# The second product of an attention kernel: seven float32 products of a 2x2 scheme, or three float32r products of 12-bit halves

## The chip, the cores and the metric

The kernel runs on one core of one Trainium2 chip. The metric is the device time of one execution in microseconds; lower is better. Input and output lie in device memory as the reference has them.

## The reference, cut to what matters

```python
x: (4, 64, 64, 256)      # B, W, H, C;  N = W*H = 4096, C2 = 128
q = einsum('bwhc,cd->bwhd', x, Wq) + bq      # C -> 128
k = einsum('bwhc,cd->bwhd', x, Wk) + bk      # C -> 128
v = einsum('bwhc,cd->bwhd', x, Wv) + bv      # C -> 256
pq, pk, pv = (t.reshape(B, -1, N) for t in (q, k, v))   # a plain reshape, no transpose
energy = einsum('bcn,bcm->bnm', pq, pk)      # 4096 x 4096 for each image, over 128
attention = softmax(energy, axis=-1)         # over m
out = einsum('bcm,bnm->bcn', pv, attention)  # 256 x 4096, over m = 4096
return gamma * out.reshape(B, W, H, C) + x   # all float32
```

For each image n are the queries, m the keys. The "first product" below is the energy, the "second product" is v times the exponentials.

## The kernel before, in words

All data is float32. A float32 matmul of the source is one call; the trace shows what it becomes.

**Projections** (class Projection, lines 99 to 166). x is loaded in 16 pieces of 128 x 2 x 256 for each image (line 78, on SyncE's queue). TensorE transposes a piece (line 122), ScalarE copies it from PSUM (line 128, tile xts), TensorE makes q and k (line 135, pieces "qk") and VectorE adds their biases (line 143) into the resident tiles pq and pk. v() (lines 150 to 166) makes a piece of v with the channels on PSUM's columns; ScalarE adds the bias (line 164).

**The order** is written out by hand (manual_schedule): each engine runs its instructions in the order of the source. Queries go in groups of 512 (NB), keys in tiles of 128; a step u is one pair of key tiles of one group, 16 steps to a group and 128 to an image. The energies (line 250: pk tile stationary, 512 queries moving) run LEAD = 18 steps ahead of the second product, so there is a buffer of 19 pairs of exponentials (ppool). ScalarE takes the exponential (line 260) without subtracting a maximum. VectorE adds the exponentials up (line 271, tile ssum); at a group's end column_sums makes the sum over the partitions by a product with ones (line 283), and reciprocals (lines 286, 300).

**The second product** (attend, line 340) uses a Strassen-like 2x2 scheme in Winograd's form: v's four blocks and the exponentials' four blocks (two key tiles, two halves of 256 queries) are combined to seven products instead of eight. left_side (lines 236 to 243, GpSimd) makes the combinations of v once for each image, right_side (lines 305 to 319, VectorE) those of the exponentials in each step. The left side is stationary (128 x 128), the right one moves (256 columns). The second half of the queries is scaled by a ratio w of the column sums before (line 312), so that the two halves can be mixed. Seven sums accumulate in four PSUM banks over the 16 steps of a group. finish (lines 351 to 380) copies them (line 354, ScalarE), combines them, scales by gamma over the column sum (line 376), adds x (line 378) and writes the result on GpSimd's queue (line 379). It is a generator whose pieces are handed out by proceed(), two in each step.

The image after is projected (project_qk) in the last 18 steps of an image, in which no energies are left to make; v follows in the lead-in of the next one, between its energies. At the end, four VectorE operations (lines 409 to 412) test the column sums against bounds (Z_LOW, Z_HIGH, line 62), and a general branch (from line 416, with the maximum subtracted) would compute everything again where they don't hold.

Of the kernel before, what the change touches and what calls it, by code (L numbers as in the profile page):

```python
# [8 lines left out]
F32 = mybir.dt.float32  # L9
I32 = mybir.dt.int32  # L10
AF = mybir.ActivationFunctionType
# [6 lines left out]
def kernel(  # L18
# [43 lines left out]
    Z_LOW, Z_HIGH = 2.0**-30, 2.0**90  # L62
# [36 lines left out]
    class Projection:  # L99
# [50 lines left out]
        def v(self, i):  # L150
            pool, tag = self.psum
            vp = pool.tile([P, KC, C], F32, tag=tag, name=f"v_{self.b}_{i}")
            for eh in range(KC):
                for k in range(KC):
                    nc.tensor.matmul(  # L155
                        vp[:, eh, :],
                        wv_sb[:, k, eh * P : (eh + 1) * P],
                        self.xt[i][:, k].rearrange("p s a -> p (s a)"),
                        start=(k == 0),
                        stop=(k == KC - 1),  # L160
                    )
            to = self.v_out(i)
            for eh in range(KC):
                nc.scalar.activation(  # L164
                    to[:, eh, :], vp[:, eh, :], AF.Identity, bias=bv_sb[:, eh : eh + 1]
                )

    NB = 512
    HB = NB // 2
    NG = N // NB  # L170
    NP = NM // 2
    STEPS = NG * NP
    LEAD = NP + 2


    M2, M1, M3, M5, M6, M7, M4 = ((k // 2, k % 2) for k in range(7))
    SLOTS = [slice(0, 5, 4), slice(2, 4), slice(5, 7), slice(1, 2)]
    again = const.tile([P, 1], I32, name="again")

    zsum = const.tile([P, 2, B * NG, 2], F32, name="zsum")  # L180

    with ExitStack() as fast:
# [4 lines left out]
        xpool, qkv, apool = pool("xpool", 4), pool("qkv", 1), pool("apool", 1)  # L187

        ppool = pool("ppool", LEAD + 1)
        bpool, work, stat = pool("bpool", 2), pool("work", 1), pool("stat", 2)  # L190
        ps_s = pool("ps_s", 4, space=PSUM)
        ps_m = pool("ps_m", 1, space=PSUM)

        images, pairs, sides, left, now = [], {}, {}, {}, {}
        recip, scale = {}, {}
# [11 lines left out]
        def image(b):  # L207
            def xt_out(i):
                if i % 2 == 0:
                    now["xt"] = ppool.tile([P, 2, KC, 2, P], F32, tag="p", name=f"xts_{b}_{i}")  # L210
                return now["xt"][:, i % 2]

            def v_out(i):
                left[b, i] = apool.tile([P, 7, P], F32, tag=f"a{i}", name=f"a_{b}_{i}")
                return left[b, i][:, 0:4, :].rearrange("p (h s) c -> p h (s c)", h=2)

            pr = Projection(b, xpool, qkv, (ps_s, "s"), xt_out, v_out)
            images.append(pr)
            return pr

        def project_qk(b):
            pr = image(b)
            pr.transposed(0)
            for i in range(NI):
# [3 lines left out]
                yield  # L228

        def project_v(b):  # L230
            for i in range(NI):
                images[b].v(i)
                left_side(left[b, i])
                yield

        def left_side(a):


            tt = nc.gpsimd.tensor_tensor
            tt(a[:, 4, :], a[:, 1, :], a[:, 3, :], ALU.add)  # L240
            tt(a[:, 5, :], a[:, 4, :], a[:, 0, :], ALU.subtract)  # L241
            tt(a[:, 1, :], a[:, 0, :], a[:, 1, :], ALU.subtract)
            tt(a[:, 6, :], a[:, 2, :], a[:, 5, :], ALU.subtract)

        def energy(b, u, h):

            g, t = divmod(u, NP)
            pr = images[b]
            sp = ps_s.tile([P, NB], F32, tag="s", name=f"s_{b}_{u}_{h}")
            nc.tensor.matmul(  # L250
                sp,
                pr.pk[:, 2 * t + h, :],
                pr.pqf[:, g * NB : (g + 1) * NB],
                start=True,
                stop=True,
            )
            if h == 0:

                pairs[b, u] = ppool.tile([P, 2, 2, HB], F32, tag="p", name=f"p_{b}_{u}")
            nc.scalar.activation(  # L260
                pairs[b, u][:, h].rearrange("p f n -> p (f n)"), sp, AF.Exp
            )

        def running_sum(b, u):
            g, t = divmod(u, NP)
            flat = lambda u: pairs[b, u].rearrange("p h f n -> p h (f n)")
            if t == 0:
                now["sum"] = work.tile([P, 2, NB], F32, tag="ssum", name=f"ssum_{b}_{g}")
            else:
                q = flat(u - 1) if t == 1 else now["sum"]  # L270
                nc.vector.tensor_tensor(now["sum"], q, flat(u), ALU.add)  # L271
            if t == NP - 1:
                start(column_sums(b, g, now["sum"]))

        def column_sums(b, g, ssum):
            n = b * NG + g
            first, second = slice(0, HB), slice(HB, NB)
            z = work.tile([P, NB], F32, tag="z", name=f"z_{b}_{g}")
            nc.vector.tensor_tensor(z, ssum[:, 0, :], ssum[:, 1, :], ALU.add)
            yield  # L280
            yield
            zb = ps_s.tile([P, NB], F32, tag="s", name=f"zb_{b}_{g}")
            nc.tensor.matmul(zb, ones, z, start=True, stop=True)  # L283

            r2 = work.tile([P, HB], F32, tag="r2", name=f"r2_{b}_{g}")
            nc.vector.reciprocal(r2, zb[:, second])  # L286
            w = stat.tile([P, HB], F32, tag="w", name=f"w_{b}_{g}")
            nc.vector.tensor_tensor(w, zb[:, first], r2, ALU.mult)  # L288
            recip[b, g] = r = stat.tile([P, HB], F32, tag="r", name=f"r_{b}_{g}")
            scale[b, g] = w  # L290

            def total(j, f, t):
                nc.scalar.activation(  # L293
                    z[:, :HB], t, AF.Identity, accum_out=zsum[:, j, n, f : f + 1]
                )

            total(0, 0, zb[:, first])
            total(0, 1, zb[:, second])
            yield
            nc.vector.reciprocal(r, zb[:, first])  # L300
            total(1, 1, r2)
            yield
            total(1, 0, r)

        def right_side(b, u):

            p = pairs[b, u]
            w = scale[b, u // NP].unsqueeze(1).to_broadcast([P, 2, HB])  # L310
            tt = nc.vector.tensor_tensor
            tt(p[:, :, 1, :], p[:, :, 1, :], w, ALU.mult)  # L312
            q = bpool.tile([P, 4, HB], F32, tag="q", name=f"q_{b}_{u}")

            tt(q[:, 0:2, :], p[:, :, 1, :], p[:, 0, :, :], ALU.subtract)  # L315

            tt(q[:, 2, :], q[:, 1, :], p[:, 0, 0, :], ALU.add)  # L317
            tt(q[:, 3, :], q[:, 2, :], p[:, 1, 0, :], ALU.subtract)  # L318
            sides[b, u] = q

        def attend(b, u, part):
            g, t = divmod(u, NP)
            if t == part == 0:
                now["acc"] = [
                    ps_m.tile([P, 2, HB], F32, tag=f"m{k}", name=f"m{k}_{b}_{g}")
                    for k in range(4)
                ]
            p, q, a = pairs[b, u], sides[b, u], left[b, t]
            products = [
                (M2, 2, p[:, 1, 0, :]),  # L330
                (M1, 0, p[:, 0, 0, :]),
                (M3, 6, p[:, 1, 1, :]),
                (M5, 4, q[:, 0, :]),
                (M6, 5, q[:, 2, :]),
                (M7, 1, q[:, 1, :]),
                (M4, 3, q[:, 3, :]),
            ]
            for (bank, half), s, right in products[4 * part : 4 * part + 4]:

                nc.tensor.matmul(  # L340
                    now["acc"][bank][:, half, :],
                    a[:, s, :],
                    right,
                    start=(t == half == 0),
                    stop=(t == NP - 1),
                    skip_group_check=True,
                )
            if t == NP - 1 and part:
                start(finish(b, g, now["acc"]))

        def finish(b, g, acc):
            m = work.tile([P, 7, HB], F32, tag="m", name=f"msb_{b}_{g}")
            for bank, to in enumerate(SLOTS):
                nc.scalar.copy(m[:, to, :], acc[bank][:, : 1 if bank == 3 else 2, :])  # L354
            xr = []
            for f in range(2):
                t = xpool.tile([P, 2, XB], F32, tag="x", name=f"xr_{b}_{g}_{f}")
                nc.sync.dma_start(t, xv[b, 2 * g + f])
                xr.append(t)
            yield  # L360
            yield
# [180 lines left out]
```

## Time and profile before

| | |
|---|---|
| median of 3 runs | 2733.33 us (2733.29 to 2736.7) |
| the profiled execution's own time | 2733.03 us |
| its span in the profile | 2731.0 us, at a mean granted TensorE clock of 0.999 |
| data moved | 34.21 MB read, 16.78 MB written, 19 GB/s over the span |

The profile's engines: PE is TensorE's matmuls, PEld its weight loads, which are recorded apart, DVE is VectorE, ACT ScalarE, POOL GpSimd, SP SyncE; a name with a q behind it is the engine's queue of other instructions, and where a row names it, the issuer of a DMA. A row of a group has the line, the engine, the operation, out<-in by the program's names, the shapes (partitions x elements), how many there are, their busy time in us with the mean ns of one, then the idle time of the engine just before them and what ended most of it. A row of the timeline has the start in us, the length in us and what ran; equal instructions that follow one another are merged to one row with their count. A row of the waits has who waited for whom, us in total, times, and the longest. A row of the DMA issues ends with the KB of one and the median us from issue to landing. Matmuls are pipelined: a record lasts longer than the distance to the next one.

### The profile page before, as it was taken

What the parts mean: (1) busy time and instruction counts of PE and PEld (TensorE: products, weight loads), DVE (VectorE), ACT (ScalarE), POOL (GpSimd) and SP (SyncE); (2) the same over time, 40 slices, a digit from 0 to 9 for tenths busy, and PEclk for the clock granted to TensorE, in tenths of its full rate; (3) what the DMA queues carried; (4) which work ended last, traced back from release to release, by engine and by line L of the source; (5) the groups of instructions that cost most, each with busy time, mean ns of one, the idle gap of its engine ahead of it and who ended that gap; (6) DMA issues with size and microseconds to landing.
All of it is one profiled execution on the core that took longest, in us unless ns stands there. A gap on an engine that the chain in (4) does not pass through costs nothing.

```text
span 2731.0 us, 28069 instructions
## 1 busy us (share of the span) xinstructions
PE 2708.1 (99%) x10560; PEld 1982.2 (73%) x10560; DVE 2045.2 (75%) x3077; ACT 804.3 (29%) x1601; POOL 170.9 (6%) x326
## 2 busy tenths in 40 slices
PE   9999999999999999999999999999999999999998
PEld 6677777778767777777876777777787677777776
DVE  3687778887568777788756887778865788877787
ACT  3422322231342322232133222222213332223220
POOL 1200000000220000000022000000003100000000
PEclk9999999999999999999999999999999999999999
DMA  2000000001100000000100000000020000000000
GB/s 87 1 12 4 16 16 16 16 16 59 35 0 16 8 8 16 16 16 16 62 31 1 16 16 5 12 16 16 16 66 27 1 16 16 12 4 16 16 16 17
DMA packets 41614, 52.86 MB, mean 19 GB/s; under 512 B 3584, under 2 KB 37376, under 8 KB 41472
## 3 DMA queue, kind: packets, MB, share of 16 engines
q1 hardware_dynamic: 34816, 33.56, 4.0%
q0 software_dynamic: 5120, 16.78, 1.5%
q8 instruction: 85, 1.39, 0.2%
q10 hardware_dynamic: 1536, 0.66, 0.1%
q14 instruction: 57, 0.47, 0.1%
HBM read 34.21 MB, written 16.78 MB: 19 GB/s over the span
## 4 chain that ended last, share of the span: by engine, by line
PE 77%; issue 21%; POOL 0%; ACT 0%; DVE 0%; DMA 0%; POOLq 0%; SPq 0%; ACTq 0%
PE m L340 42%; PE s L250 25%; PE qk L135 4%; PE v L155 4%; PE xt L122 1%; PE zb L283 1%; POOL out_dram L379 0%; DVE r L286 0%; DMA x<-in_x_dram 0%; ACT a L164 0%; ACT z L293 0%; ACT xts L128 0%; DVE w L288 0%; ACT L128 0%; POOL a L241 0%
## 5 line engine op out<-in xcount | busy, mean ns | idle before, releaser
L260 ACT ACTIVATE p<-s 128x512 f32<-128x512 f32 x1024 | 606.0, 599 | 1367.8 <-PE s L250 1298.6
L340 PE MATMUL m<-q,a 128*128 128x256 f32 x4096 | 972.2, 379 | 0.0
L250 PE MATMUL s<-pq,pk 128*128 128x512 f32 x2048 | 961.0, 592 | 0.0
L340 PEld LDWEIGHTS m<-q,a 128*128 128x128 f32 x4096 | 778.2, 190 | 117.8 <-issue 13.4
L340 PEld LDWEIGHTS m<-p,a 128*128 128x128 f32 x3072 | 581.6, 190 | 272.8 <-issue 198.3
L271 DVE TENSOR_TENSOR ssum<-ssum,p 128x1024 f32<-128x1024 f32 x448 | 562.7, 1256 | 272.0 <-ACT p L260 272.0
L340 PE MATMUL m<-p,a 128*128 128x256 f32 x3072 | 746.9, 379 | 3.2 <-ACT msb L354 3.2
L250 PEld LDWEIGHTS s<-pq,pk 128*128 128x128 f32 x2048 | 389.1, 190 | 274.8 <-issue 245.9
L315 DVE TENSOR_TENSOR q<-p 128x512 f32<-128x512 f32 x512 | 355.1, 694 | 212.7 <-PE m L340 189.5
L312 DVE TENSOR_TENSOR p<-p,w 128x512 f32<-128x512 f32 x512 | 349.9, 683 | 1.1
L318 DVE TENSOR_TENSOR q<-q,p 128x256 f32<-128x256 f32 x512 | 219.2, 428 | 17.6
L317 DVE TENSOR_TENSOR q<-q,p 128x256 f32<-128x256 f32 x512 | 218.1, 426 | 17.4
L379 POOL DMA_DIRECT2D out_dram<-xr x64 | 44.2, 690 | 2404.8 <-DVE xr L378 2143.7
L155 PEld LDWEIGHTS v<-xts,wv_sb 128*128 128x128 f32 x512 | 96.9, 190 | 44.6 <-ACT a L164 18.4
L135 PE MATMUL qk<-wqk_sb,xts 128*128 128x256 f32 x512 | 122.9, 384 | 1.9 <-ACT xts L128 1.9
L155 PE MATMUL v<-xts,wv_sb 128*128 128x256 f32 x512 | 121.4, 380 | 2.7 <-ACT a L164 2.7
L286 DVE RECIPROCAL r<-zb 128x256 f32<-128x256 f32 x32 | 56.3, 1758 | 70.1 <-PE zb L283 70.1
L135 PEld LDWEIGHTS qk<-wqk_sb,xts 128*128 128x128 f32 x512 | 93.7, 192 | 13.5 <-ACT xts L128 3.0
L128 ACT COPY xts<-xt 128x512 f32<-128x512 f32 x64 | 37.3, 589 | 191.4 <-PE xt L122 191.4
L354 ACT COPY msb<-m 128x512 f32<-128x512 f32 (+1 forms) x128 | 59.0, 536 | 85.9 <-PE m L340 85.9
L164 ACT ACTIVATE a<-v,bv_sb 128x256 f32<-128x256 f32 x128 | 53.6, 470 | 65.8 <-PE v L155 65.8
L143 DVE TENSOR_TENSOR pq<-qk,bqk_sb 128x256 f32<-128x256 f32 x64 | 27.1, 424 | 55.5 <-PE qk L135 55.1
(36 smaller groups left out, 660.0 us busy)
## 6 DMA issues: line engine op xcount, KB each, us to landing
x<-in_x_dram SPq DMA_DIRECT2D x64, 256.0 KB, 2.9
xr<-in_x_dram SPq DMA_DIRECT2D x64, 256.0 KB, 2.8
out_dram<-xr POOLq DMA_DIRECT2D x64, 256.0 KB, 2.4
wv_sb<-in_L_conv_Wv_dram ACTq DMA_DIRECT2D x1, 256.0 KB, 5.2
wqk_sb<-in_L_conv_Wq_dram ACTq DMA_DIRECT2D x1, 128.0 KB, 2.1
wqk_sb<-in_L_conv_Wk_dram ACTq DMA_DIRECT2D x1, 128.0 KB, 3.2
bqk_sb<-in_L_conv_bq_dram ACTq DMA_DIRECT2D x1, 64.0 KB, 5.6
bqk_sb<-in_L_conv_bk_dram ACTq DMA_DIRECT2D x1, 64.0 KB, 6.0
```

The source lines that it names most:

```text
L135: nc.tensor.matmul(qk[:, s, :], self.xt[i][:, k, s, :], wqk_sb[:, k, :], start=(k == 0), stop=(k == KC - 1),)
L155: nc.tensor.matmul(vp[:, eh, :], wv_sb[:, k, eh * P : (eh + 1) * P], self.xt[i][:, k].rearrange("p s a -> p (s a)"), start=(k == 0), stop= ...
L250: nc.tensor.matmul(sp, pr.pk[:, 2 * t + h, :], pr.pqf[:, g * NB : (g + 1) * NB], start=True, stop=True,)
L260: nc.scalar.activation(pairs[b, u][:, h].rearrange("p f n -> p (f n)"), sp, AF.Exp)
L271: nc.vector.tensor_tensor(now["sum"], q, flat(u), ALU.add)
L286: nc.vector.reciprocal(r2, zb[:, second])
L312: tt(p[:, :, 1, :], p[:, :, 1, :], w, ALU.mult)
L315: tt(q[:, 0:2, :], p[:, :, 1, :], p[:, 0, :, :], ALU.subtract)
L317: tt(q[:, 2, :], q[:, 1, :], p[:, 0, 0, :], ALU.add)
L318: tt(q[:, 3, :], q[:, 2, :], p[:, 1, 0, :], ALU.subtract)
L340: nc.tensor.matmul(now["acc"][bank][:, half, :], a[:, s, :], right, start=(t == half == 0), stop=(t == NP - 1), skip_group_check=True,)
L354: nc.scalar.copy(m[:, to, :], acc[bank][:, : 1 if bank == 3 else 2, :])
```

## The change

The diff takes out the 2x2 scheme (left_side, right_side, running_sum, column_sums, the long lead and its buffers) and computes the second product from halves. Each number x of the exponentials is split into h, a copy scaled by just under 1 and written as float32r (a 4-byte type whose values are cut to 12 bits of mantissa when an engine writes them), and what is left of it. v is split in the same way. With E = 2^-12 the four half products are got from three sums, by Karatsuba's identity: a = sum of h*vh and of l*vl (vl is scaled by 1/E), b = sum of d*vd with d = h*E - l and vd = (v - vh)/E - vh. Then a*(1 + E) + b is the whole product.

The exponentials are now stationary (128 keys x 128 queries) and v moves (256 channels). vh and vl have two columns of ones behind the 256 channels, so that column 256 of a is the column sum. A group is 256 queries (NB = 256), a unit u four key tiles; there are 16 groups of 8 units for each image. The energies run LOOK = 2 units ahead; their matmuls stay float32 and move 256 columns. For each unit ScalarE makes two exponentials of 128 x 512 and the cut copy of 128 x 1024, VectorE two passes over 128 x 1024 (l and d). Four accumulators (a and b for each of two blocks of 128 queries) take one PSUM bank each, once. As the result now has the queries on the partitions, finish transposes it by four TensorE transposes before x is added.

Each image is projected as a whole before its energies, with v's piece three behind q and k's (LAG = 3). The bounds Z_LOW and Z_HIGH become 2^-60 and 2^80, and the test at the end adds a small product with ones over the partitions. The general branch stays as it was.

The diff, cut to its core (the lines marked + are added; what they replace is printed above):

```diff
+            v4 = now["v4"]
+            h = vh[:, m, :C]
+            nc.scalar.activation(h, v4, AF.Identity, scale=UPPER * E)
+            for t, f in ((vl, 1.0 / E), (vd, 1.0 / E + 1.0)):
+                nc.vector.scalar_tensor_tensor(
+                    t[:, m, :C], h.bitcast(F32), -f, v4, ALU.mult, ALU.add
+                )
...
+        def energy(b, u):
+            g, t = divmod(u, NU)
+            pr = images[b]
+            x = ppool.tile([P, 4, NB], F32, tag="x", name=f"x_{b}_{u}")
+            for k in range(2):
+                sp = ps_s.tile([P, 2, NB], F32, tag="s", name=f"s_{b}_{u}_{k}")
+                for i in range(2):
+                    nc.tensor.matmul(sp[:, i, :], pr.pk[:, 4 * t + 2 * k + i, :],
+                        pr.pqf[:, g * NB : (g + 1) * NB], start=True, stop=True)
+                nc.scalar.activation(x[:, 2 * k : 2 * k + 2, :], sp, AF.Exp)
+            h = ppool.tile([P, 4, NB], F32R, tag="h", name=f"h_{b}_{u}", bufs=LOOK + 1)
+            nc.scalar.activation(h, x, AF.Identity, scale=UPPER)
+        def halves(b, u):
+            x, h = units[b, u]
+            l = ppool.tile([P, 4, NB], F32R, tag="l", name=f"l_{b}_{u}")
+            nc.vector.tensor_tensor(l, x, h.bitcast(F32), ALU.subtract)
+            d = ppool.tile([P, 4, NB], F32R, tag="d", name=f"d_{b}_{u}")
+            nc.vector.scalar_tensor_tensor(
+                d, h.bitcast(F32), 1.0 + E, x, ALU.mult, ALU.subtract)
+        def attend(b, u):
...
+            for j in range(NJ):
+                a, bb = now["acc"][j]
+                for i in range(4):
+                    m = 4 * t + i
+                    n = slice(j * P, (j + 1) * P)
+                    for out_, left, right, first, last in (
+                        (a, h, vh, True, False),
+                        (a, l, vl, False, True),
+                        (bb, d, vd, True, True),
+                    ):
+                        nc.tensor.matmul(out_, left[:, i, n], right[:, m, :],
+                            start=(m == 0 and first), stop=(m == NM - 1 and last))
+        def finish(b, g, acc):
+            xr = load_x(xpool, b, g)
...
+            for j in range(NJ):
+                a, bb = acc[j]
+                nc.vector.tensor_copy(z[:, j : j + 1], a[:, C : C + 1])
+                nc.vector.reciprocal(r[:, 0, j : j + 1], z[:, j : j + 1])
+                nc.vector.tensor_tensor(r[:, 0, j : j + 1], r[:, 0, j : j + 1], gam, ALU.mult)
+                nc.vector.tensor_scalar(r[:, 1, j : j + 1], r[:, 0, j : j + 1], 1.0 + E, None, ALU.mult)
+                nc.scalar.activation(o[:, j, :], bb, AF.Identity, scale=r[:, 0, j : j + 1])
+                nc.vector.scalar_tensor_tensor(
+                    o[:, j, :], a[:, :C], r[:, 1, j : j + 1], o[:, j, :], ALU.mult, ALU.add)
+            yield
+            yield
+            tp = ps_s.tile([P, 2, NB], F32, tag="s", name=f"ot_{b}_{g}")
+            for s in range(2):
+                for j in range(NJ):
+                    nc.tensor.transpose(
+                        tp[:, s, j * P : (j + 1) * P], o[:, j, s * P : (s + 1) * P], ident)
+            nc.vector.tensor_tensor(xr, xr, tp, ALU.add)
+            nc.gpsimd.dma_start(ov[b, g], xr)
+        for b in range(B):
+            image(b)
+            pr = images[b]
             pr.transposed(0)
             for i in range(NI):
                 if i + 1 < NI:
                     pr.transposed(i + 1)
                 pr.qk(i)
+                if i >= LAG:
+                    project_v(b, i - LAG)
+                proceed()
+            energy(b, 0)
+            for i in range(NI - LAG, NI):
+                project_v(b, i)
+            for u in range(1, LOOK):
+                energy(b, u)
+            halves(b, 0)
+            for u in range(STEPS):
+                if u + LOOK < STEPS:
+                    energy(b, u + LOOK)
+                proceed()
+                if u + 1 < STEPS:
+                    halves(b, u + 1)
+                attend(b, u)
+                proceed()
```

More of the change, by code (lines that the diff above doesn't have):

```diff
@@ L9 @@
 F32 = mybir.dt.float32
+F32R = mybir.dt.float32r
 I32 = mybir.dt.int32
@@ L161, in v @@
                     )
-            to = self.v_out(i)
+            to, bias, scale = self.v_out(i)
             for eh in range(KC):
                 nc.scalar.activation(
-                    to[:, eh, :], vp[:, eh, :], AF.Identity, bias=bv_sb[:, eh : eh + 1]
-                )
-    NB = 512
-    HB = NB // 2
+                    to[:, eh, :],
+                    vp[:, eh, :],
+                    AF.Identity,
+                    bias=bias[:, eh : eh + 1],
+                    scale=scale,
+                )
+    NB = 256
+    NJ = NB // P
     NG = N // NB
[L171 to L177, printed above, removed]
+    NU = NM // 4
+    STEPS = NG * NU
+    LOOK = 2
+    LAG = 3
+    E = 2.0**-12
+    UPPER = 1.0 - 2.0**-13
     again = const.tile([P, 1], I32, name="again")
-    zsum = const.tile([P, 2, B * NG, 2], F32, name="zsum")
+    zall = const.tile([P, B * NG, NJ], F32, name="zall")
+    bv4_sb = const.tile([P, KC], F32, name="bv4_sb")
+    nc.scalar.mul(bv4_sb, bv_sb, 1.0 / E)
     with ExitStack() as fast:
@@ L218, in image, with project_v @@
[L218 to L222, printed above, removed]
+                now["v4"] = work.tile([P, KC, C], F32, tag="v4", name=f"v4_{b}_{i}")
+                return now["v4"], bv4_sb, 1.0 / E
+            images.append(Projection(b, xpool, qkv, (ps_s, "s"), xt_out, v_out))
+        def project_v(b, i):
+            images[b].v(i)
+            v4 = now["v4"]
+            m = slice(2 * i, 2 * i + 2)
+            h = vh[:, m, :C]
[4 more added lines that the diff above has]
+                )
@@ new lines, in halves @@
+        def halves(b, u):
[4 more added lines that the diff above has]
+            nc.vector.scalar_tensor_tensor(
+                d, h.bitcast(F32), 1.0 + E, x, ALU.mult, ALU.subtract
+            )
+            units[b, u] = h, l, d
+        def attend(b, u):
+            g, t = divmod(u, NU)
+            if t == 0:
+                now["acc"] = [
+                    (
+                        ps_o.tile([P, C + 2], F32, tag=f"a{j}", name=f"a{j}_{b}_{g}"),
+                        ps_o.tile([P, C], F32, tag=f"b{j}", name=f"b{j}_{b}_{g}"),
+                    )
+                    for j in range(NJ)
+                ]
+            h, l, d = units[b, u]
+            for j in range(NJ):
[8 more added lines that the diff above has]
+                    ):
+                        nc.tensor.matmul(
+                            out_,
+                            left[:, i, n],
+                            right[:, m, :],
+                            start=(m == 0 and first),
+                            stop=(m == NM - 1 and last),
+                        )
+            if t == NU - 1:
+                start(finish(b, g, now["acc"]))
@@ L227, in project_qk @@
                 pr.qk(i)
[L228 to L349, printed above, removed]
@@ L382 @@
-        for _ in project_qk(0):
-            pass
-        for b in range(B):
-            values = project_v(b)
-            for u in range(-LEAD, STEPS):
-                if u == STEPS - LEAD:
-                    ahead = project_qk(b + 1) if b + 1 < B else iter(())
-                if 0 <= u + 1 < STEPS:
-                    right_side(b, u + 1)
-                if u + LEAD < STEPS:
-                    energy(b, u + LEAD, 0)
-                    energy(b, u + LEAD, 1)
-                else:
-                    next(ahead, None)
-                for part in range(2):
-                    proceed()
-                    if u >= 0:
-                        attend(b, u, part)
-                    elif part and u >= -NP:
-                        next(values, None)
-                if u + LEAD < STEPS:
-                    running_sum(b, u + LEAD)
+                if i >= LAG:
+                    project_v(b, i - LAG)
@@ L408 @@
     zs = const.tile([P, 2], F32, name="zs")
-    nc.vector.tensor_reduce(zs, zsum.rearrange("p j n f -> p j (n f)"), AX.X, ALU.max)
-    nc.vector.tensor_scalar(zs[:, 0:1], zs[:, 0:1], Z_HIGH, None, ALU.is_gt)
-    nc.vector.tensor_scalar(zs[:, 1:2], zs[:, 1:2], 1.0 / Z_LOW, None, ALU.is_gt)
-    nc.vector.tensor_tensor(again, zs[:, 0:1], zs[:, 1:2], ALU.add)
+    zf = zall.rearrange("p n j -> p (n j)")
+    nc.vector.tensor_reduce(zs[:, 0:1], zf, AX.X, ALU.min)
+    nc.vector.tensor_reduce(zs[:, 1:2], zf, AX.X, ALU.max)
+    nc.vector.tensor_scalar(zs[:, 0:1], zs[:, 0:1], Z_LOW, None, ALU.is_lt)
+    nc.vector.tensor_scalar(zs[:, 1:2], zs[:, 1:2], Z_HIGH, None, ALU.is_gt)
+    nc.vector.tensor_tensor(zs[:, 0:1], zs[:, 0:1], zs[:, 1:2], ALU.add)
+    with tc.tile_pool(name="ps_z", bufs=1, space=PSUM) as ps_z:
+        zp = ps_z.tile([P, 1], F32, name="zp")
+        nc.tensor.matmul(zp, ones, zs[:, 0:1], start=True, stop=True)
+        nc.vector.tensor_copy(again, zp)
+    NB = 512
+    NG = N // NB
     NJ = NB // P
+    NP = NM // 2
     xg, og = columns(x, NB), columns(out, NB)
@@ L432 @@
                 lambda i: xtpool.tile([P, KC, 2, P], F32, tag="xt", name=f"gxt_{b}_{i}"),
-                lambda i: pvT[:, 2 * i : 2 * i + 2, :],
+                lambda i: (pvT[:, 2 * i : 2 * i + 2, :], bv_sb, 1.0),
             )
```

77 lines of the change are left out of this document (35 added, 42 removed).

## The prediction

> **What bounds the kernel now.** I read the page's busy times first, then what TensorE waited for.
>
> ```profile
> span 2731.0 us, 28069 instructions
> ...
> PE 2708.1 (99%) x10560; PEld 1982.2 (73%) x10560; DVE 2045.2 (75%) x3077; ACT 804.3 (29%) x1601; POOL 170.9 (6%) x326
> ...
> PEclk9999999999999999999999999999999999999999
> ```
>
> ```profile
> PE xt L122 <- DMA x<-in_x_dram: 5.3, 2, 4.2
> PE m L340 <- ACT msb L354: 3.2, 1, 3.2
> PE v L155 <- ACT a L164: 2.7, 4, 0.7
> PE qk L135 <- ACT xts L128: 1.9, 4, 1.2
> ```
>
> TensorE waits 13.1 us in all (first numbers of the four rows), at the full clock. Nothing else can be late by much: the time is the sum of what TensorE issues. A busy time of pipelined matmuls isn't their price, so the price comes from the timeline, start to start. Two stretches of it, TensorE's matmuls, then (third fence) its weight loads in the second stretch:
>
> ```profile
> 999.52 1.89 PE L340 MATMUL m<-q,a 128*128 128x256 f32 x8
> 1001.25 1.88 PE L250 MATMUL s<-pq,pk 128*128 128x512 f32 x4
> 1002.96 0.38 PE L340 MATMUL m<-p,a 128*128 128x256 f32 x1
> ```
>
> ```profile
> 33.70 0.60 PE L122 MATMUL xt<-ident,x 128*128 128x128 f32 x4
> 34.14 0.38 PE L135 MATMUL qk<-wqk_sb,xts 128*128 128x256 f32 x1
> ```
>
> ```profile
> 33.49 0.57 PEld L122 LDWEIGHTS xt<-ident,x 128*128 128x128 f32 x4
> 34.03 0.30 PEld L135 LDWEIGHTS qk<-wqk_sb,xts 128*128 128x128 f32 x2
> ```
>
> Eight records of 256 columns start in 1001.25 - 999.52 = 1.73 us, 216 ns each; four of 512 in 1.71 us, 429 each; four transposes of 128 columns in 0.44 us, 109 each. All fit 0.42 ns a beat, two beats to a column, and 2.5 ns. Now the counts:
>
> ```profile
> L340 PE MATMUL m<-q,a 128*128 128x256 f32 x4096 | 972.2, 379 | 0.0
> L250 PE MATMUL s<-pq,pk 128*128 128x512 f32 x2048 | 961.0, 592 | 0.0
> L340 PEld LDWEIGHTS m<-q,a 128*128 128x128 f32 x4096 | 778.2, 190 | 117.8 <-issue 13.4
> L340 PE MATMUL m<-p,a 128*128 128x256 f32 x3072 | 746.9, 379 | 3.2 <-ACT msb L354 3.2
> L135 PE MATMUL qk<-wqk_sb,xts 128*128 128x256 f32 x512 | 122.9, 384 | 1.9 <-ACT xts L128 1.9
> L155 PE MATMUL v<-xts,wv_sb 128*128 128x256 f32 x512 | 121.4, 380 | 2.7 <-ACT a L164 2.7
> L122 PE MATMUL xt<-ident,x 128*128 128x128 f32 x256 | 38.9, 278 | 5.3 <-DMA x<-in_x_dram 5.3
> L283 PE MATMUL zb<-z,ones 128*128 128x512 f32 x64 | 32.7, 592 | 0.0
> L122 PEld LDWEIGHTS xt<-ident,x 128*128 128x128 f32 x256 | 32.3, 143 | 11.7 <-issue 4.1 <-DMA x<-in_x_dram 1.5
> ```
>
> The source issues 512 x 7 = 3584 products at L340, and the trace has 4096 + 3072 = 7168 records: each float32 product is two records, 2 x 216 = 432 ns. The sum: 7168 x 216 = 1548 us, 2048 x 429 = 879, 1024 x 216 = 221, 256 x 109 = 28, 64 x 429 = 27: 2704 of 2731 us. Head, tail and waits are the other 27.
>
> **The second product.** Removed are its 7168 records (1548 us). Added are, for each of 512 units (a query block of 256 against 4 key tiles), 2 x 4 x 3 = 24 float32r products of 256 or 258 columns: 12,288. No row shows one. From above, it costs what a float32 record of 256 columns costs, 216 ns; from below 109, the shortest spacing of any load and matmul pair here. I take 109.6: 256 beats at one beat a column, with two columns more in two of three. The reason is an estimate from the rows: if the 432 ns of a float32 product are four products of half operands, one is 108, and an operand cut to 12 bits leaves one. So 12,288 x 109.6 = 1347 us, 201 less than before.
>
> The Trainium skill (FP8 and Floating Point Precision, TensorE Precision Notes) says that true float32 takes four passes through the array, and that a reduced precision reads four bytes and truncates to FP22. By it the price would be 108 too; that float32r is this mode, no run here shows.
>
> The new stationary operand changes with every product, so a load must fit into 109 ns, and its record lasts 190 (143 for a transpose). The transposes do it: 109 apart with 143 ns loads. At the handover the load for qk starts at 34.03 and its matmul at 34.14, 110 ns on, in the middle of the 190. So the record's length is no pace. Unequal overlap may cost a few ns: 113 instead of 109.6 adds 42 us, kept for the range.
>
> **The rest of TensorE.** Energies: 4096 records of 256 columns, 4096 x 216 = 885, 6 more. Projections and transposes stay (221 + 28). 64 column-sum records (27) go; 256 output transposes come (28). The column of ones is in the 258. Sum 1347 + 885 + 221 + 28 + 28 = 2509 us.
>
> **The other engines.** A unit is 8 x 216 + 24 x 109.6 = 4.36 us of TensorE.
>
> ```profile
> L260 ACT ACTIVATE p<-s 128x512 f32<-128x512 f32 x1024 | 606.0, 599 | 1367.8 <-PE s L250 1298.6 <-DVE p L312 68.9
> L271 DVE TENSOR_TENSOR ssum<-ssum,p 128x1024 f32<-128x1024 f32 x448 | 562.7, 1256 | 272.0 <-ACT p L260 272.0
> L164 ACT ACTIVATE a<-v,bv_sb 128x256 f32<-128x256 f32 x128 | 53.6, 470 | 65.8 <-PE v L155 65.8
> L376 DVE SCALAR_TENSOR_TENSOR msb<-msb,gam,r 128x512 f32<-128x512 f32 x64 | 47.7, 745 | 0.0
> L378 DVE TENSOR_TENSOR xr<-xr,msb 128x512 f32<-128x512 f32 x64 | 44.7, 698 | 2.2
> L128 ACT COPY xts<-xt 128x512 f32<-128x512 f32 x64 | 37.3, 589 | 191.4 <-PE xt L122 191.4
> L410 DVE TENSOR_SCALAR zs<-zs 128x1 f32<-128x1 f32 x1 | 0.1, 148 | 0.0
> ```
>
> VectorE has two passes over 1024 elements, about 1.26 and 1.3 us (the fused form is 745 to 698 at 512): 2.6 of 4.36. ScalarE has two exponentials of 0.6 and a scaled copy of 1024, under 1.2 as two of 512: 2.4 of 4.36. Buffers allow the lead: exp of unit u+2 runs under unit u, and its x buffer came free a unit before; l and d of u+1 are made under u and wanted 1.7 us after it ends. So they cost nothing until an engine's share doubles nearly. Removed right_side, running sums, reciprocals of 256 and the GpSimd sums were hidden too and give nothing back.
>
> What isn't hidden is a group's end, 63 times. The accumulators are single; TensorE has 8 x 0.216 = 1.73 us of energy first, then the four output transposes, which stand ahead of the next attend and wait for o[1]. That needs per j three small VectorE steps in a chain (0.15 each and some 0.04 between: 0.57), ScalarE 0.47, a fused VectorE pass over 256 (about 0.47), hand-overs of 0.1. j=0 starts 1.3 us before TensorE ends and is through 0.65 after; j=1 runs behind it on VectorE, 1.8 us more: o[1] at 2.45 after, 0.7 later than the energies. 63 x 0.7 = 44 us; with 0.2 to 1.3, 13 to 82. Then the xr add (0.7) and halves follow on VectorE with about 1 us to spare.
>
> Images are no longer projected under the tail of the one before. At a new image TensorE waits for the first xts copy behind o[1] (1.3 us), and for VectorE, which at the phase's end has the last v halves before the first l and d (2.2).
>
> ```profile
> x<-in_x_dram SPq DMA_DIRECT2D x64, 256.0 KB, 2.9
> ...
> out_dram<-xr POOLq DMA_DIRECT2D x64, 256.0 KB, 2.4
> ```
>
> On SP's queue, the fourth x load takes the buffer of the last xr and so waits for that group's output: add at about 5.7 us after the boundary, issue on POOL's queue and landing 2.4, load 2.9: 11, where the transposes want it near 6.6. That is 4.4 more, 8 us for each of three images, and 2 for the first: 26 in all (8 to 40).
>
> ```profile
> 8.64 3.57 PE L135 MATMUL qk<-wqk_sb,xts 128*128 128x256 f32 x8 [1.16 <-ACT xts L128]
> 12.04 0.60 PE L122 MATMUL xt<-ident,x 128*128 128x128 f32 x4
> ```
>
> ```profile
> 2719.22 1.89 PE L340 MATMUL m<-q,a 128*128 128x256 f32 x8
> ```
>
> Head: 8.64 us until the first projection less 0.87 of transposes in it, and eight records in 3.40 instead of 1.73: 9.5, plus 0.5 for the scaled bias on ScalarE's queue ahead of the first copy: 10. Tail: 10 now (2731.0 less the end of the last stream at 2720.95); one shorter chain, 9. The general branch isn't entered: from the reference's inputs the column sums lie between 2^26.8 and 2^69.2, inside the new bounds.
>
> Sum: 2509 + 44 + 26 + 10 + 9 = 2598 of span. The profiled execution took 2733.03 us, 2.0 above its span and 0.3 below the median of the runs, so 2600 us.
>
> **The rivals.** (1) *A float32r product still takes two beats a column*, as every record of this trace does, the transposes too: 216 ns. 12,288 x 216 = 2654 instead of 1347: 3907 us. It turns slower from the point where the spacing passes 109.6 + (2733 - 2600)/12,288 = 120.4 ns. For it: no record here streams faster. Against it: the float32 products are in two records already, so something is split that halves needn't be. If the products were even run as full float32, two records each, it would be about 6560 us.
>
> (2) *The weight load sets the pace.* If a matmul must wait for the whole record of its load, the spacing is about 190 ns (2340 us, 3590 in all) or 143 (1757, 3010). Against it stands the 110 ns handover; for it, that no run of such short matmuls behind 190 ns loads is shown. A stricter form has load and matmul strictly in turn: at least 143 + 109.6 = 253 ns, 4360 us. The loads that are hidden at 216 and 109 ns above speak against that. The Trainium skill (TensorE: Matmul & The Clock Gate, What overlaps and what doesn't) states that weight loads overlap running matmuls only where the row group differs, which would be this form; the trace disagrees, since all its loads fill 128 rows and are hidden.
>
> (3) *The same, with heavy edges*: boundaries at 1.5 us or more, VectorE or ScalarE slower in writing float32r. The slack of a unit is 1.8 us, so a VectorE pass would have to reach 2.2 us. Ends near 2710, no change.
>
> **The numbers.** Forecast 0.82; rival 1 0.07; rival 2 0.05 (0.01 of it the stricter form); rival 3 0.06, a third of it within 0.2%. From the bounds: 2540 (13 at groups, 8 at images, 109.0 a product) to 2690 (113 a product, 82 at groups, 40 at images: 2694). Two in ten lie outside, most on the slow side. About 0.2% is what a measurement of this kernel tells from no change. Faster 0.86, same 0.02, slower 0.12.
>
> **What would show it.** A run of attend records 109 to 110 ns apart, one record for each product (12,288); TensorE waiting for o at the output transposes, 0.2 to 1.3 us, 63 times; TensorE waiting for an x load three times. Records 216 apart, or 24,576 of them, show rival 1; loads that end just before each matmul starts, rival 2; TensorE waiting for h, l or d in mid-group would mean that the cover of VectorE or ScalarE was overrated.

## The result and the profile after

The changed kernel takes 2665.7 us (median of 4 runs, 2664.96 to 2666.91) where the kernel before takes 2735.01 beside it: a ratio of 0.9746, 95% interval 0.9729 to 0.9763, 2.5% faster. The forecast was 2600 us, the range 2540 to 2690. The direction and the range held, but half of the forecast gain of 133 us is missing, and the profile says where. First the page of the kernel after, its span and busy times:

```profile
span 2665.1 us, 42006 instructions
...
PE 2639.4 (99%) x17922; PEld 2486.4 (93%) x17922; DVE 1506.8 (57%) x1993; ACT 1333.7 (50%) x1922; POOL 44.8 (2%) x70
```

TensorE is still the bound. VectorE and ScalarE are at about half, as worked out. The groups, in the kernel after:

```profile
L294 PE MATMUL a<-vh,h 128*128 128x258 f32 x4096 | 1242.3, 303 | 0.0
L294 PE MATMUL a<-vl,l 128*128 128x258 f32 x4096 | 1156.2, 282 | 1.9 <-DVE l L265 1.9
L294 PE MATMUL b<-vd,d 128*128 128x256 f32 x4096 | 1151.3, 281 | 3.0 <-DVE d L268 3.0
L250 PE MATMUL s<-pq,pk 128*128 128x256 f32 x4096 | 966.5, 379 | 0.0
L294 PEld LDWEIGHTS a<-vh,h 128*128 128x128 f32 x4096 | 773.6, 189 | 11.5
L265 DVE TENSOR_TENSOR l<-x,h 128x1024 fp32r<-128x1024 f32 x512 | 626.5, 1224 | 844.4 <-issue 841.8
L268 DVE SCALAR_TENSOR_TENSOR d<-h,x 128x1024 fp32r<-128x1024 f32 x512 | 623.9, 1219 | 0.0
L259 ACT ACTIVATE h<-x 128x1024 fp32r<-128x1024 f32 x512 | 542.7, 1060 | 16.3
L330 PE MATMUL ot<-ident,o 128*128 128x128 f32 x256 | 45.6, 286 | 1.5 <-DVE o L322 1.2 <-DVE zall L311 0.3
```

There are 3 x 4096 = 12,288 records for 12,288 products: float32r is one record each, not two. (The trace writes "f32" for the type of these operands.) How far apart they are, the timeline shows; a stretch of it in mid-group, TensorE's matmuls of the kernel after:

```profile
1205.94 0.28 PE L294 MATMUL a<-vl,l 128*128 128x258 f32 x1
1206.06 0.28 PE L294 MATMUL b<-vd,d 128*128 128x256 f32 x1
1206.17 0.28 PE L294 MATMUL a<-vh,h 128*128 128x258 f32 x1
1206.29 0.28 PE L294 MATMUL a<-vl,l 128*128 128x258 f32 x1
1206.41 0.28 PE L294 MATMUL b<-vd,d 128*128 128x256 f32 x1
1206.53 1.89 PE L250 MATMUL s<-pq,pk 128*128 128x256 f32 x8
1208.07 0.47 PE L294 MATMUL a<-vh,h 128*128 128x258 f32 x1
```

From 1205.94 to 1206.53 five matmuls: 118 ns each, not 109.6. From the start of the energies of one unit to that of the next it is 4.58 us, as in another stretch:

```profile
98.93 1.89 PE L250 MATMUL s<-pq,pk 128*128 128x256 f32 x8
...
103.51 1.89 PE L250 MATMUL s<-pq,pk 128*128 128x256 f32 x8
```

So the second product takes 4.58 - 8 x 0.216 = 2.85 us for 24, 119 ns each. No row names a wait in between. (The row at 1208.07 starts early in the records, 1.54 us after the energies instead of 1.73, and lasts longer for it; the next one is at its place.) What TensorE did wait for, in the kernel after, then a wait of its weight loads and one of ScalarE:

```profile
PE qk L136 <- ACT xts L129: 7.7, 4, 5.2
PE xt L123 <- DMA x<-in_x_dram: 4.0, 1, 4.0
PE b L294 <- DVE d L268: 3.0, 4, 0.8
PE a L294 <- DVE l L265: 1.9, 4, 0.5
PE ot L330 <- DVE o L322: 1.2, 1, 1.2
PE zp L374 <- DVE x L333: 0.8, 1, 0.8
```

```profile
PEld ot L330 <- DVE o L322: 15.8, 61, 1.4
ACT L189 <- DMA bv_sb<-in_L_conv_bv_dram: 9.4, 1, 9.4
```

The group's end, in the kernel after (TensorE, then VectorE's last step of o):

```profile
926.98 1.89 PE L250 MATMUL s<-pq,pk 128*128 128x256 f32 x8
928.71 0.72 PE L330 MATMUL ot<-ident,o 128*128 128x128 f32 x4
...
932.12 0.38 PE L250 MATMUL s<-pq,pk 128*128 128x256 f32 x1
```

```profile
927.19 0.15 DVE L311 COPY zall<-a 128x1 f32<-128x1 f32 x1
927.37 0.16 DVE L312 RECIPROCAL r<-zall 128x1 f32<-128x1 f32 x1
927.57 0.16 DVE L313 TENSOR_TENSOR r<-r,gam 128x1 f32<-128x1 f32 x1
...
928.33 0.48 DVE L322 SCALAR_TENSOR_TENSOR o<-a,r,o 128x256 f32<-128x256 f32 x1 [0.41 <-ACT o L319]
```

A unit with a group's end takes 932.12 - 926.98 = 5.14 us, 0.56 more than the others, of which the transposes are 4 x 0.109 = 0.44. The wait for o is 0.12 us, not 0.7: o is ready at 928.81, 1.83 us after the group's last product, and the energies have covered 1.73 of it.

### The profile page after: what moved, and what is told of

Same layout as the page of the kernel before. It is cut to its first block, busy times and chain, and to the rows that moved or that the text cites. A ratio compares the mean times of both kernels' runs of the same rounds, so it can differ in the third digit from the quotient of the medians.

```text
span 2665.1 us, 42006 instructions
## 1 busy us (share of the span) xinstructions
PE 2639.4 (99%) x17922; PEld 2486.4 (93%) x17922; DVE 1506.8 (57%) x1993; ACT 1333.7 (50%) x1922; POOL 44.8 (2%) x70
## 4 chain that ended last, share of the span: by engine, by line
PE 98%; DVE 1%; ACT 0%; DMA 0%; issue 0%; POOL 0%; ACTq 0%
PE a L294 37%; PE s L250 33%; PE b L294 18%; PE qk L136 4%; PE v L156 4%; PE ot L330 1%; PE xt L123 1%; DMA bv_sb<-in_L_conv_bv_dram 0%; DVE d L268 0%; DVE l L265 0%; ACT v L165 0%; ACT o L319 0%; DMA wqk_sb<-in_L_conv_Wk_dram 0%; DVE vl L238 0%; ACT vh L235 0%; DVE o L322 0%
## 5 line engine op out<-in xcount | busy, mean ns | idle before, releaser
L294 PE MATMUL a<-vh,h 128*128 128x258 f32 x4096 | 1242.3, 303 | 0.0
L294 PE MATMUL a<-vl,l 128*128 128x258 f32 x4096 | 1156.2, 282 | 1.9 <-DVE l L265 1.9
L294 PE MATMUL b<-vd,d 128*128 128x256 f32 x4096 | 1151.3, 281 | 3.0 <-DVE d L268 3.0
L257 ACT ACTIVATE x<-s 128x512 f32<-128x512 f32 x1024 | 610.5, 597 | 1056.2 <-PE s L250 1042.6
L265 DVE TENSOR_TENSOR l<-x,h 128x1024 fp32r<-128x1024 f32 x512 | 626.5, 1224 | 844.4 <-issue 841.8
L250 PE MATMUL s<-pq,pk 128*128 128x256 f32 x4096 | 966.5, 379 | 0.0
L294 PEld LDWEIGHTS a<-vl,l 128*128 128x128 f32 x4096 | 773.1, 189 | 14.5 <-DVE l L265 3.1
L294 PEld LDWEIGHTS a<-vh,h 128*128 128x128 f32 x4096 | 773.6, 189 | 11.5
L294 PEld LDWEIGHTS b<-vd,d 128*128 128x128 f32 x4096 | 774.0, 189 | 3.8 <-DVE d L268 3.8
L268 DVE SCALAR_TENSOR_TENSOR d<-h,x 128x1024 fp32r<-128x1024 f32 x512 | 623.9, 1219 | 0.0
```

Source lines behind the costliest of these rows:

```text
L250: nc.tensor.matmul(sp[:, i, :], pr.pk[:, 4 * t + 2 * k + i, :], pr.pqf[:, g * NB : (g + 1) * NB], start=True, stop=True,)
L257: nc.scalar.activation(x[:, 2 * k : 2 * k + 2, :], sp, AF.Exp)
L265: nc.vector.tensor_tensor(l, x, h.bitcast(F32), ALU.subtract)
L268: nc.vector.scalar_tensor_tensor(d, h.bitcast(F32), 1.0 + E, x, ALU.mult, ALU.subtract)
L294: nc.tensor.matmul(out_, left[:, i, n], right[:, m, :], start=(m == 0 and first), stop=(m == NM - 1 and last),)
```

## The experiments

Theory A: loading the stationary operand sets the pace of float32r matmuls. Theory B: each float32r matmul has some 10 ns on top of its columns, whatever is loaded. Others are named where they come up. The spans below are to be set against 2665.1 us; where no median is given, the run is one execution.

**512 columns a matmul.** The edit (and the columns of ones left out):

```diff
-                for i in range(4):
+                for i in range(0, 4, 2):
...
-                            right[:, m, :],
+                            right[:, m : m + 2, :],
```

> The second product moves 512 columns a matmul (two key tiles of v side by side) with half as many matmuls, 12 a unit; half of the products and the columns of ones are left out, and the column sum is a constant. Theory A (the load of the stationary operand sets the pace: some 119 ns from one float32r matmul's start to the next, whatever it moves up to about 280 columns): matmuls of 512 columns are 216 ns apart, as float32 records with 512 beats are; a unit 8 x 216 + 12 x 216 = 4.32 us instead of 4.59, the span about 2530 us. Theory B (each float32r matmul has about 12 ns on top of its columns): 225 ns apart, a unit 4.43 us, the span about 2585 us.

Measured: a span of 2593.7 us. Its timeline in mid-group, TensorE:

```profile
1205.07 0.39 PE L292 MATMUL b<-vd,d 128*128 128x512 f32 x1
1205.30 0.39 PE L292 MATMUL a<-vh,h 128*128 128x512 f32 x1
1205.53 0.39 PE L292 MATMUL a<-vl,l 128*128 128x512 f32 x1
...
1207.12 0.39 PE L292 MATMUL b<-vd,d 128*128 128x512 f32 x1
1207.34 1.89 PE L248 MATMUL s<-pq,pk 128*128 128x256 f32 x8
```

Ten matmuls in 1207.34 - 1205.07 = 2.27 us, 227 ns each; 216 was theory A's value. The load of 188 ns had long ended when such a matmul did, and still there are 11 ns on top. Theory A falls; the cost is one for each matmul and hardly grows with its columns (9 ns over the 109.6 for 256 or 258, 11 over the 216 for 512).

**bfloat16 halves.** The one line F32R = mybir.dt.float32r becomes mybir.dt.bfloat16 (and the bitcasts go).

> The halves of the exponentials and of v are bfloat16 instead of float32r, so the stationary operand is 2 bytes an element; the precision is lost. The counts and columns are those of the changed kernel. Theory A: the load is shorter, its record well under 189 ns, and the moving operand sets the pace: 109 to 110 ns apart, the span about 12,288 x 9.4 ns = 115 us shorter, 2550 us. Theory B, or a bound from the issue of two instructions a matmul (59 ns each): 119 ns apart as before, 2660 us, with a shorter load record.

Measured: a span of 2559.7 us. Its timeline, TensorE:

```profile
1206.37 0.27 PE L294 MATMUL a<-vh,h 128*128 128x258 bf16 x1
1206.48 0.27 PE L294 MATMUL a<-vl,l 128*128 128x258 bf16 x1
...
1209.00 1.89 PE L250 MATMUL s<-pq,pk 128*128 128x256 f32 x8
```

From 1206.37 to 1209.00 there are 24 matmuls, 109.6 ns each, exactly the price that the prediction gave to float32r. The load's record is 98 ns here. So neither the issue of two instructions for each product nor the accumulators nor the order of the work costs the 9 ns: the type does. The Trainium skill (TensorE: Matmul & The Clock Gate, Back-to-back issue gap) gives N / 2.4 + 2.5 ns as the isolated gap of a matmul of N columns, which makes 109.2 for 256 and 215.8 for 512; for a stream of pairs of load and matmul it has other figures, about 131 ns for 512. The bfloat16 run, a stream of such pairs, agrees with the formula; float32r agrees with neither, with 119 and 227.

**No columns of ones.** The tiles vh, vl and the accumulator lose their two columns.

> The columns of ones are left out, so all second products move 256 columns from rows of 1024 bytes, and the column sum is a constant. Theory A: spacing unchanged at 118 to 119 ns, the span within 10 us of 2665. If the two columns more, or rows that start off a multiple of 1024 bytes, cost the 9 ns: 109 ns, about 2550 us. Theory B: 0.8 ns less for two of three, 7 us less in all.

Measured: a span of 2664.5 us. In the timeline the spacing is 120 ns (from 1205.92 to 1207.24, eleven matmuls). Neither the two columns nor the rows of 1032 bytes are the cause. That the span is the same is two small differences that cancel: a unit without a group's end takes 4.60 us here instead of 4.58, and one with it 5.03 instead of 5.14, where the chain to o no longer starts with a copy out of the accumulator.

**64 stationary columns.**

```diff
-                    n = slice(j * P, (j + 1) * P)
+                    n = slice(j * P, j * P + P // 2)
```

> Only 64 of the 128 stationary columns are used in the second product (half of the queries are left out, their outputs are x alone; the column sum is a constant). Moving columns and counts are unchanged. Theory B1 (the 10 to 12 ns that a float32r matmul takes on top of its columns belong to taking over a stationary operand of 4 bytes, in proportion to its columns): the record of the load gets shorter than 189 ns and the spacing falls to about 114 ns, the span to about 2600 us. Theory B2 (the 10 ns belong to each float32r matmul, whatever is loaded): the spacing stays at 118 to 120 ns, the span at 2665 us within 10.

Measured: a span of 2640.6 us, between the two. The loads and the matmuls of this run:

```profile
L294 PEld LDWEIGHTS a<-vh,h x4096: 133/134/138, 82.8 to 2630.6; 128*64 128x64 f32 x196
L294 PE MATMUL a<-vh,h x4096: 277/280/470, 82.8 to 2630.7; 128*64 128x258 f32 x196
```

```profile
1204.77 0.28 PE L294 MATMUL b<-vd,d 128*64 128x256 f32 x1
...
1206.65 1.89 PE L250 MATMUL s<-pq,pk 128*128 128x256 f32 x8
```

The load's record is 134 ns (minimum/median/maximum in the row) instead of 188, and 16 matmuls take 1.88 us: 117.5 ns each. Half of the load takes 1 to 1.5 ns off, where theory B1 wanted 5. The bulk stays with the matmul, as theory B2 has it. Not all of the 24.5 us of span is the load's: a unit with a group's end takes 4.97 us here instead of 5.14, 10 us over 60 groups, in a run that also leaves out the column sum.

**One VectorE pass twice.**

```diff
-            nc.vector.tensor_tensor(l, x, h.bitcast(F32), ALU.subtract)
+            for _ in range(2):
+                nc.vector.tensor_tensor(l, x, h.bitcast(F32), ALU.subtract)
```

> The VectorE pass that makes l is done twice: 1.22 us more VectorE work in each unit, 3.66 of 4.59 us. If VectorE is covered with slack, as the prediction said: the span stays within 5 us of 2665. If the halves are nearly late, in mid-group or behind the group's end: some 10 to 60 us more, with TensorE waiting for l or d.

Measured: a span of 2704.6 us, 39.5 more. The expectation of no cost was wrong, for the most part at one place. The group's end in this run, TensorE:

```profile
941.85 1.89 PE L250 MATMUL s<-pq,pk 128*128 128x256 f32 x8
943.57 0.27 PE L331 MATMUL ot<-ident,o 128*128 128x128 f32 x1
944.19 0.55 PE L331 MATMUL ot<-ident,o 128*128 128x128 f32 x3 [0.34 <-DVE o L323]
...
947.43 0.38 PE L250 MATMUL s<-pq,pk 128*128 128x256 f32 x1
```

A unit with a group's end takes 947.43 - 941.85 = 5.58 us, 0.44 more than in the kernel after, 28 us for 63 of them. In the other units the energies still start 4.58 us apart. So VectorE is covered in mid-group even at 78% busy, but at the group's end its queue holds this chain back: its first step waited for the group's last products for 50.9 us in all in the kernel after, and for 5.7 here, so here it comes late itself. TensorE also waits longer for the first l and d of the images (12.4 us in all, 4.9 in the kernel after).

In this run the granted clock was 0.50 in two stretches of 3.4 us, which cost about 3 of the 39.5 us. They show one thing more: in the first of them fourteen float32r matmuls start in 89.10 - 86.09 = 3.01 us, 215 ns each. A beat is (429 - 216) / 512 = 0.416 ns at the full clock, so 256 to 258 columns at half of it take 213 to 215 ns. What a float32r matmul has on top at the full clock is not seen there.

**The transposes a piece later.** One more yield ahead of them in finish.

> The output transposes of a group come one piece later, after the second product of the next unit instead of ahead of it, so that o has long been ready. If TensorE's wait for o at the transposes (15.8 us for the loads in the profile after) is on the path: 12 to 18 us shorter, about 2650 us. If it is hidden by something else: within 3 us of 2665.

Measured: 2661.9 us (median of 5; ratio to the kernel before 0.9737, interval 0.9723 to 0.9750), a span of 2659.9. Against the kernel after the two intervals overlap; the profile shows the gain where it was sought. The weight load's 61 waits for o (15.8 us in the kernel after) are down to one of 1.4 us, and the transposes are 273 ns long instead of 286:

```profile
L331 PE MATMUL ot<-ident,o 128*128 128x128 f32 x256 | 38.7, 273 | 1.5 <-DVE o L322 1.2 <-DVE zall L311 0.3
```

That is 5 us of span (3.8 between the medians), not 12 to 18, and little more than the 3 us of the other expectation. The 15.8 us were waits of the weight load, and most of them lay under the running energies, where they cost TensorE nothing: a unit with transposes takes 5.03 us instead of 5.14, 6.6 us over 60 groups.

**Three direct passes, in both products.** The core of the edit, in the second product and in the energies:

```diff
-                        (a, h, vh, True, False),
-                        (a, l, vl, False, True),
-                        (bb, d, vd, True, True),
+                        (a, h, vh, True, False),
+                        (a[:, :C], h, vl, False, False),
+                        (a, l, vh, False, True),
...
+                    for p, (left, right) in enumerate(
+                        ((pr.kh, pr.qhf), (pr.kl, pr.qhf), (pr.kh, pr.qlf))
+                    ):
+                        nc.tensor.matmul(sp[:, i, :], left[:, m, :], right[:, n],
+                                         start=(p == 0), stop=(p == 2))
```

q and k are split in the projections as v is; the transposes are a piece later, as in the run before.

> The energies too are made from halves, in three float32r passes of 256 columns (kh*qh + kl*qh + kh*ql), and the second product in three direct passes (h*vh + h*vl + l*vh, all in one accumulator, twice buffered): the product of the two low halves, below 2^-24 of the whole, is left out in both, d, vd and b are gone. By the measured 119 ns a float32r matmul: energies 2048 x 3 x 119 = 731 us instead of 884, second product as now, so about 150 us less, 5 to 10 less at the group ends: a span near 2505 us. If the 119 were made by the alternation of accumulators (a, a, b) or by d: 109 ns, and some 120 us less on top.

Measured: 2523.3 us (median of 5), a ratio of 0.9226 to the kernel before, interval 0.9214 to 0.9239; a span of 2521.7, 17 more than the sum. The spacing is 120 ns in both products; from the first row here to the second there are 16 matmuls of the second product, 121 ns each:

```profile
1204.78 0.28 PE L303 MATMUL a<-vh,l 128*128 128x258 f32 x1
...
1206.71 0.28 PE L271 MATMUL s<-qh,kh 128*128 128x256 f32 x1
```

So the alternation of accumulators, and d, are not the cause of the 119 either. The energies gained as a float32 product of two records at 216 against three at 120 should: 432 - 360 = 72 ns for each of 2048, 147 us.

**The same with 512 columns.** v is stationary, and 512 queries move:

```diff
+                for s in range(2):
+                    e = slice(s * P, (s + 1) * P)
+                    for p, (left, right) in enumerate(((vh, h), (vl, h), (vh, l))):
+                        nc.tensor.matmul(now["acc"][s], left[:, m, e], right[:, k, :],
+                            start=(m == 0 and p == 0), stop=(m == NM - 1 and p == 2))
```

> As the run before (three direct float32r passes in both products), but v is stationary and 512 queries move, the energies move 512 too, and the column sums come from VectorE's running sum and a product with ones, so no output transposes: 1024 x 3 matmuls for the energies and 1024 x 6 for the second product. With 12 ns on top of 512 columns, 227 ns each as measured with 512 moving: 9216 x 227 = 2092 us, projections and transposes 260, column sums 27, edges 35: a span near 2415 us. If the on-top cost vanished with v's halves stationary: 216 each, 100 us less.

Measured: 2434.8 us (median of 5), a ratio of 0.8903 to the kernel before, interval 0.8890 to 0.8915: the fastest of all, 11% below the kernel before. Its groups of the second product and of the energies, and TensorE's largest wait:

```profile
L318 PE MATMUL a<-h,vh 128*128 128x512 f32 x2048 | 809.8, 395 | 0.0
L266 PE MATMUL s<-qh,kh 128*128 128x512 f32 x1024 | 400.3, 391 | 0.0
```

```profile
PE v L176 <- DVE t L153: 13.7, 19, 1.1
```

The matmuls are 227 ns apart here too (eleven from 1204.79 to 1207.29), so the 11 ns are paid for 512 columns instead of 256: 9216 x (2 x 120 - 227) = 120 us less than in the run before, of which 89 are left in the span. The output transposes are gone (256 x 109 ns = 28 us), but the products for the column sums are back (64 records of 512 columns, as much). Against the kernel before, an energy of 512 columns costs 3 x 227 = 681 ns instead of 2 x 429 = 858. The span is 2432.9 us, 18 over the sum; 13.7 of these are TensorE's wait for VectorE in the projections, where q and k are now split.

## Why the prediction was right, and where it was off

The terms beside what they came to, in us:

| term | forecast | after | from |
|---|---|---|---|
| second product, 12,288 float32r | 1347 | 1462 | 119 ns each |
| energies | 885 | 885 | 216 ns each |
| projections and input transposes | 249 | 249 | as before |
| output transposes and the wait for o | 72 | 35 | 63 x 0.56 |
| starts of the images | 26 | 7 | waits: 3.0 + 1.9 + 2.5 |
| head and tail | 19 | 27 | the rest of the span |
| span | 2598 | 2665 | |

**float32r streams one beat a column.** Right, and it decided the sign: rival 1 (216 ns) and rival 2 (143 to 190 ns) are refuted by 119 ns in the kernel after and 227 with 512 columns. That float32r keeps 12 bits of a value, on which the halves are built, no run here measures.

**The size of that term** was off: 109.6 was taken from bounds of 109 and 216, and 113 was the most allowed in the range. The step that failed is "256 beats at one beat a column" with the 2.5 ns that float32 records have on top. A float32r matmul of 256 or 258 columns has about 12 ns on top, 2.5 of which are in the 109.6: 12,288 x 9.4 = 115 us. The runs exclude the columns of ones, the issue, the accumulators, VectorE's work beside (the spacing in mid-group is the same with VectorE at 57% and 78%) and, but for 1 to 1.5 ns, the length of the load. A float32 energy that follows a float32r product also starts late (1206.41 to 1206.53, 120 ns), and a float32 product behind another doesn't, which speaks for an extra that goes with the float32r matmul that runs, and against one for taking over the next operand. What in it takes the time stays open; it isn't there at half the clock, and it was not tried to change only the moving or only the stationary operand's type, or to let two matmuls share one load.

**The loads hidden behind short matmuls.** Right: records of 189 ns every 119 ns.

**The break-even point.** 120.4 ns was worked out for the spacing at which the change gives nothing. At 119 it still gave 69 us, because the other terms came out 48 us lower. Without that the change would have gained 21 us.

**The group's end.** Right in kind: after nearly every group the transposes' load waits for o (61 times). The forecast was 0.7 us of TensorE, the trace has 0.12. The chain for j=1 takes 928.81 - 927.19 = 1.62 us, where 1.8 was reckoned, and j=0 was through 0.3 us after the group's last product instead of 0.65. The run with a doubled VectorE pass shows that this was luck of a few tenths: 0.44 more there. So it isn't right either that VectorE's passes cost nothing until its share nearly doubles: from 57% to 78% busy cost 28 us at the groups' ends.

**The image's start.** The waits for the first copy and for the first l and d came (2.5 and 4.9 us). The step that failed is that "the fourth x load takes the buffer of the last xr and so waits for that group's output". Six of SyncE's DMAs in the kernel after start like this, with the output of the last group below:

```profile
672.97 9.41 SPq L79 DMA_DIRECT2D x<-in_x_dram  x6
```

```profile
677.86 0.69 POOL L334 DMA_DIRECT2D out_dram<-x  x1 [35.17 <-DVE x L333]
```

The new image's first three loads were out long before (at 570.08, 607.31 and 644.57). The fourth is the first of the six in the row: it goes out at 672.97, as the transposes of the first piece end, 4.9 us ahead of that output. The one that waits for the output is the eighth, at 680.79, and TensorE has no wait for x after the kernel's start (one row, once, 4.0 us). So the fourth load took the buffer of the first piece, not that of the last xr.

**The head.** 0.5 us was given to the scaled bias on ScalarE's queue. The waits have ScalarE held for 9.4 us by the bias's DMA at that place, ahead of the first copy, and the first projection starts at 11.45 us instead of 8.64, 2.8 later.

**The general branch** wasn't entered, and VectorE and ScalarE took 1.22 + 1.22 and 1.06 us for what was put at 1.26, 1.3 and 1.2: right.

## What to carry to other kernels

Price a matmul type that the trace doesn't have from a short run of that type before a sum is built on it: an error of 9 ns in 110 was 115 us of a forecast gain of 133 here, because 12,288 of them stood on the path, and only the other terms gave 48 back. A cost that each matmul has on top of its columns is spread by more columns: 512 instead of 256 moved columns gave 5% on every float32r matmul (2 x 119 to 227). And where halves are split anyway, three direct passes into one accumulator, without the product of the low halves, need a third less splitting work than the Karatsuba form (1.06 + 1.22 us a unit, without the second 1.22) and serve the energies too.

## What the runs showed of the hardware

- A float32r matmul is one record; 119 ns for 256 or 258 moving columns, 227 for 512. float32 is two records, 432 ns for 256 and 858 for 512. bfloat16 has 109.6 for 256 or 258. At a granted clock of 0.50 float32r has 215 for 256 or 258, with nothing to be seen on top of its columns.
- The load of 128 stationary columns has a record of 189 ns in float32r, as in float32, and 98 in bfloat16; with 64 columns of float32r it is 134. Behind matmuls 119 ns apart they are hidden, but for 1 to 1.5 ns at most.
- VectorE's passes that write float32r take 1224 ns for 1024 elements, no more than a float32 sum (1220 beside 1219 in the last run); ScalarE's take 1060.
